# Four decoder layers on one core: moving the maxima of two attentions and the first block of two expert layers

## The chip, the cores and the metric

The kernel runs on one core of a Trainium2 chip. The metric is the device time of one execution in microseconds (us); several executions are made and their median is taken. The engines are TensorE (PE, its weight loads are shown as PEld), VectorE (DVE), ScalarE (ACT), GpSimd (POOL) and SyncE (SP, which only issues DMAs here). Each works through its own instructions in order and waits on semaphores for the others.

## The reference

`x` has 8 batches of 256 tokens with 128 features, `ctx` 8 batches of 1601 tokens with 64. Four layers of cross attention and feed-forward follow each other, each on the layer norm of x and added to it. Shortened:

```python
x = x + attention0(layernorm(x), ctx)   # 16 heads of 8, softmax over 1601 keys
x = x + ffn0(layernorm(x))              # attention among the 16 heads of a token, then a
                                        # mixture: sum over 8 experts e of gate[e] * (h2 @ We[e])
x = x + attention1(layernorm(x), ctx)   # 16 heads of 64
x = x + ffn1(layernorm(x))              # quantised linear, convolution of 3 taps, silu, linear
x = x + attention2(layernorm(x), ctx)   # one head of 128, no output projection
x = x + ffn2(layernorm(x))              # 8 experts, routed: sum of w[t,e] * down(silu(gate) * up)
x = x + attention3(layernorm(x), ctx)   # 16 heads of 8
x = x + ffn3(layernorm(x))              # 32 routed experts (8 of 32 a token) and a shared one
```

## The kernel before

All of it is one program of one core in five stages, written in the order in which each engine is to work: `attn0` (with ffn0 of batch 0 beside its last units), `wide` (attentions 1 and 2, with ffn0 of the other batches, ffn1 and the preparation of weights beside them), `experts` for ffn2, `attn3`, `experts` for ffn3.

**Attentions 0 and 3** are the function `narrow`. The work is 8 batches of 4 *units*, each unit being 4 heads of one batch; n counts the units, 0 to 31. A unit has 7 pairs of key chunks and two head groups, hence 14 *half steps*. In each, PE makes scores (`score`, L1011), ACT their exponentials (L1014), PE multiplies those of the step before with V (`values`, L1023). The softmax needs the maximum of every row beforehand: `maxima(n)` gives 14 tasks (`pair`), each two matmuls of a head pair's queries with a piece of the keys into banks of the pool `m` (three banks, L813) and two maximum reductions on DVE (L816); 2 of the 14 tasks are the short last pieces. A 15th task, `shift`, turns the maxima into a negated row; `place_shift(n)` transposes it on PE (L834) and has SP write it into Q (L838). `place(n, t)` has SP and POOL write K and Q of unit n into a ring of four. In unit n the tasks of unit n + 2 are spread over the 14 half steps; in unit 0 those of unit 1 come ahead of those of unit 2. The list `beside` holds other work with its place in the unit as a fraction.

Outside that list, at the end of `narrow`, the last batch's attention is divided by its sums, projected and added (`finish`, L846 to L854).

**Attentions 1 and 2** are the function `wide`: 272 jobs, 256 of attention 1 (32 a batch: 16 heads, 2 halves of the tokens) and 16 of attention 2 (2 a batch). A job n makes scores and maxima of n + 1, transposes the exponentials of n (`turn`), projects and adds n - 1, and multiplies the exponentials with v (`values`). Other work stands in `beside[n]`: what its steps have under "pe", "act0" and "dve" is issued ahead of `values`, what they have under "act" and "pool" behind it. The pool `m`, from which these steps and the queries take their PSUM, has one bank. ffn0 of batch b has 26 steps beside the 32 jobs of batch b - 1; its steps 22 to 25 are the mixture (four matmuls, and after each four multiply-adds of DVE into X, L1223). ffn1 of a batch follows in the next 32 jobs, that of batch 7 in jobs 256 to 266, one step a job. `prepare3` fetches the weights of ffn3 (`fetch`), turns them (`turn`, L1725) and writes them to DRAM, in jobs 27 to 31 of batches 1 to 6; `flip` and `maps2` are small transposes and maps that follow it there.

**The experts** work on 4 blocks k of 512 tokens. `prepare(k)` makes the layer norm, its transpose yT (L1613, L1615), the routing (L1619 to L1630, a sigmoid on ACT, many small DVE operations) and its transpose combT (L1634, L1636). `hidden(k, c)` makes gate and up of 128 hidden features (L1642, L1643), Silu on ACT and a product on DVE; six jobs later `weigh` (L1651) multiplies by the routing weights, and `down` (L1657) follows. For k = 0 `prepare` runs at the start of the stage, with its arithmetic on DVE; for the other blocks it runs beside the jobs of the block before.

Of the kernel before, what the change touches and what calls it, by code (L numbers as in the profile page):

```python
# [42 lines left out]
NB = 8  # L43
# [8 lines left out]
RING = 4  # L52
AFTER = 26
# [3 lines left out]
def decoder_kernel(ctx: ExitStack, tc: tile.TileContext, a: dict, out: bass.AP):  # L57
# [283 lines left out]


# [9 lines left out]
    def wide(layers, before, extra):  # L352
# [11 lines left out]
        with ExitStack() as es:  # L364
# [152 lines left out]
            beside = extra(es, A, B, bias)  # L517
# [114 lines left out]
    def narrow(wq, wkT, wvT, wo, bq, bk, bv, bo, first, after=None):  # L632
# [8 lines left out]
        with ExitStack() as es:  # L641
# [215 lines left out]
            class Scratch:  # L857

                PARTS = (("ct", KW), ("raw", NC * DC), ("nat", 512), ("nat", 512), ("k", 512), ("k", 512))
                SAME = dict(f0_h2="f0_h", f0_h2T="f0_hT", f0_mixT="f0_q", f0_y2="f0_dT")  # L860

                def __init__(self):
                    self.whole = [((one if t == "ct" else two).tile([P, n], F32, tag=t, name=f"left_{t}",
                                                                    bufs=1 if t in ("ct", "raw") else 2), n)
                                  for t, n in self.PARTS]
                    self.free = [n for _, n in self.PARTS]
                    self.at = {}

                def tile(self, shape, dt, tag=None, name=None, bufs=None):
                    n = 1  # L870
                    for x in shape[1:]:
                        n *= x
                    tag = self.SAME.get(tag or name, tag or name)
                    if tag not in self.at:

                        i = min((i for i in range(len(self.free)) if self.free[i] >= n), key=lambda i: self.free[i])
                        self.at[tag] = i, self.PARTS[i][1] - self.free[i], n
                        self.free[i] -= n
                    i, at, room = self.at[tag]
                    assert n <= room  # L880
                    t = self.whole[i][0][0:shape[0], at:at + n]
                    if len(shape) > 2:
                        axes = " ".join(f"a{x}" for x in range(len(shape) - 1))
                        t = t.rearrange(f"p ({axes}) -> p {axes}", **{f"a{x}": v for x, v in enumerate(shape[1:])})
                    return t
# [68 lines left out]
            more = maxima(1)  # L954
            for n in range(units):
                b, i = divmod(n, 4)
                v = V[b % 2]

                ms = []
                if n == 0:  # L960
                    ms += [*more[0], more[1]]
                if n + 2 < units:
                    pairs, shift = maxima(n + 2)
                    ms += [*pairs, shift]
                due = [len(ms) * (x + 1) // (2 * steps) for x in range(2 * steps)]
                done = 0
# [5 lines left out]
                if n + 1 < units:  # L972
                    beside.append((1.0 if n == 0 else 0.1, lambda: place_shift(n + 1)))
# [17 lines left out]
                if after is not None and n >= AFTER:  # L991
                    if n == AFTER:
                        late = after(Scratch(), bank)
                    per = 2 * steps
                    beside += [((x - per * (n - AFTER)) / per, lambda x=x: run([late[x]], EARLY + LATE))
                               for x in late if x // per == n - AFTER]
# [35 lines left out]
                for p in range(steps):  # L1032
                    e = two.tile([P, 4, 2, LQ], F32, tag="e", name="e")
                    for t in range(2):
                        score(p, t, e)
                        if before:
                            before.pop(0)()
                        while beside and (beside[0][0] * 2 * steps < 2 * p + t + 1 or p * t == steps - 1):
                            beside.pop(0)[1]()
                        for f in ms[done:due[2 * p + t]]:  # L1040
                            f()
                        done = due[2 * p + t]
# [22 lines left out]

    def attn3():
# [7 lines left out]
        with tc.tile_pool(name="w3", bufs=1) as p:  # L1074
# [4 lines left out]
            narrow(w3qT, flipped(0), flipped(1), w3oT, None, None, None, None, False)  # L1079


    def ffn0(p, b, bank=pm):
# [137 lines left out]

        def weigh(j, i):
            for e in range(4):
                nc.vector.scalar_tensor_tensor(X[b][:, j, :], t["pt"][:, e * D:(e + 1) * D],  # L1223
                                               t["gate"][:, j, 4 * i + e:4 * i + e + 1], X[b][:, j, :],
                                               ALU.mult, ALU.add)

# [4 lines left out]
        def exponent(name, s):  # L1231
# [21 lines left out]
                     dve=lambda: (inverse("gate"), combine(nc.vector, "gate", E, ALU.mult), weigh(0, 0))),  # L1253
        }
        for k, (j, i) in ((23, (0, 1)), (24, (1, 0)), (25, (1, 1))):
            steps[k] = dict(pe=lambda j=j, i=i: mixture(j, i), dve=lambda j=j, i=i: weigh(j, i))
# [48 lines left out]
    def ffn1(p, b):  # L1305
# [66 lines left out]
        def tanh():  # L1372
            t["th"] = p.tile([P, 4, LQ], F32, tag="f1_th", name="f1_th")
            nc.scalar.activation(t["th"], t["h"], AF.Tanh, scale=0.5)
# [33 lines left out]
        def done():  # L1408
            for j in range(QT):
# [7 lines left out]
                dict(pe=lambda: up(1), act0=lambda: middle(1), dve=lambda: sides(1)),  # L1417
                dict(act=tanh, pool=twice_silu),
# [8 lines left out]
    def besides(es, A, B, bias):  # L1427
# [9 lines left out]
        for n, f in zip(room, prepare3() + maps2(p, p, A[1], B[1], bias)):  # L1437
            at[n] = [dict(pe=f)]
        at[32 * (NB - 1) + 14] = at.get(32 * (NB - 1) + 14, []) + [dict(pool=lambda: big.update(sel2=select2()))]
# [100 lines left out]

    y0T = const.tile([P, LQ], F32, name="y0T")
# [23 lines left out]
    def experts(wr, n_r, route, n_e, wg, wu, wd, sel, shared):  # L1565
# [6 lines left out]
        with ExitStack() as es:  # L1572
# [4 lines left out]
            halves = [one.tile([P, T, P], F32R, name=f"halves{i}") for i in range(2)]  # L1577
            for t in halves:
                nc.vector.memset(t.bitcast(F32), 0.0)
# [4 lines left out]
            yT, combT, act, o = {}, {}, {}, {}  # L1584

            def prepare(k):

                fast = k == 0
                eng = nc.vector if fast else nc.gpsimd
                tokens = [X[2 * k + t // QT][:, t % QT, :] for t in range(T)]  # L1590
                st = p.tile([P, T, 6], F32, name="st")
                mv = p.tile([P, T, 2], F32, name="mv")
                var = p.tile([P, T], F32, name="var")
                for t in range(T):
                    nc.vector.bn_stats(st[:, t, :], tokens[t])
                if not fast:
                    yield
                for t in range(T):
                    nc.vector.bn_aggr(mv[:, t, :], st[:, t, :])
                nc.vector.tensor_scalar(var, mv[:, :, 1], 1e-5, None, ALU.add)  # L1600
                rs = guess(p, var, "ex_rs")
                refine(p, rs, var, "ex_t", eng)
                if not fast:
                    yield
                y = p.tile([P, T, D], F32, name="y")
                for t in range(T):
                    eng.tensor_scalar(y[:, t, :], tokens[t], mv[:, t, 0:1], rs[:, t:t + 1], ALU.subtract, ALU.mult)
                if not fast:
                    yield
                    yield  # L1610
                pt = pm()
                for t in range(T):
                    nc.tensor.transpose(pt[:, t * P:(t + 1) * P], y[:, t, :], ident)  # L1613
                yT[k] = p.tile([P, W], F32, name="yT")
                nc.scalar.copy(yT[k], pt)  # L1615
                yield
                pt = pm()
                for t in range(T):
                    nc.tensor.matmul(pt[:, t * n_r:(t + 1) * n_r], lhsT=yT[k][:, t * P:(t + 1) * P], rhs=wr,  # L1619
                                     start=True, stop=True)  # L1620
                s = p.tile([P, T, n_r], F32, name="s")
                nc.scalar.activation(s, pt[:, 0:T * n_r].rearrange("p (t n) -> p t n", n=n_r), AF.Sigmoid)
                yield
                for comb in route(p, s):
                    if comb is None:
                        yield
                h = halves[k % 2]
                hi, lo = h[:, :, 0:n_e], h[:, :, 32:32 + n_e]
                nc.gpsimd.tensor_copy(hi, comb)
                nc.gpsimd.tensor_tensor(lo, comb, hi.bitcast(F32), ALU.subtract)  # L1630
                yield
                pt = pm()
                for t in range(T):
                    nc.tensor.transpose(pt[:, t * P:(t + 1) * P], h[:, t, :].bitcast(F32), ident)  # L1634
                combT[k] = p.tile([P, W], F32R, name="combT")
                nc.scalar.copy(combT[k], pt)  # L1636
                yield

            def hidden(k, c):
                g, u, _, _ = chunks[c]  # L1640
                gu = ps2("gu")
                nc.tensor.matmul(gu[:, 0, :], lhsT=g, rhs=yT[k], start=True, stop=True)  # L1642
                nc.tensor.matmul(gu[:, 1, :], lhsT=u, rhs=yT[k], start=True, stop=True)  # L1643
# [4 lines left out]
            def weigh(k, c):  # L1648
                if chunks[c][3] is not None:
                    cm = pm()  # L1650
                    nc.tensor.matmul(cm, lhsT=chunks[c][3], rhs=combT[k], start=True, stop=True)  # L1651
# [24 lines left out]
            ahead = prepare(0)  # L1676
            while 0 not in yT:
# [122 lines left out]
```

## Time and profile before

| what | us |
|---|---|
| median of 3 runs | 3637.28 (3630.37 to 3639.38) |
| profiled execution | 3634.52, span 3632.8 |
| PE busy | 3431.8 (94% of the span) |
| DVE busy | 2602.2 (72%) |
| ACT busy | 2281.5 (63%) |
| POOL busy | 1129.4 (31%) |
| attention 0: first scores to end of last values | 49.0 to 731.4 |
| attentions 1 and 2: first scores to last projection | 766.1 to 2493.8 |
| experts of ffn2: first to last hidden and down | 2501.7 to 2702.4 |
| attention 3: first scores to end of last values | 2742.1 to 3395.3 |
| experts of ffn3: first hidden to last down | 3409.9 to 3627.5 |

A profile is of one execution. Its times start at the first instruction. A line of a timeline gives start, duration, engine, source line, operation, the tiles written and read, shapes and a count of merged instructions; in brackets stands how long the engine had been idle before, and which engine and line released it. The granted clock is the share of TensorE's full rate that the chip granted in a stretch. A busy PE is not a PE at full rate: matmuls overlap and their ends are modelled.

### The profile page before, as it was taken

How to read it: one execution, taken by the hardware profiler on the slowest of the kernel's cores; microseconds unless marked ns; L12 is line 12 of the kernel's file. 1: busy time of each engine (PE TensorE's matmuls, PEld its weight loads, DVE VectorE, ACT ScalarE, POOL GpSimd, SP SyncE). 2: the span in 40 equal slices, each digit the busy share in tenths (PEclk: the TensorE clock that was granted, in tenths of full speed). 3: DMA queues.
4: the chain of work that ended last, by engine and by line, in shares of the span. 5: the costliest groups of instructions: out<-in, count | busy, mean ns of one | idle time of the engine just before them, and what ended most of it. 6: DMA issues, size and time to landing. Idle time of an engine off the chain costs nothing.

```text
span 3632.8 us, 74838 instructions
## 1 busy us (share of the span) xinstructions
PE 3431.8 (94%) x28363; PEld 2315.0 (64%) x28363; DVE 2602.2 (72%) x6564; ACT 2281.5 (63%) x5685; POOL 1129.4 (31%) x2007
## 2 busy tenths in 40 slices
PE   7999999979999999999999999988999999999799
PEld 4555555458787877788777788865444555555344
DVE  6788888657777767767777777675556888889365
ACT  3788887746665656666676766653223878888422
POOL 5343444614152513333150502020123333332100
PEclk6899999989999999999999999998985999999899
DMA  4445444130001001000000000020013444443100
GB/s 93 73 76 76 68 70 62 24 81 2 15 2 32 1 24 38 1 27 1 15 1 15 1 15 1 11 69 18 0 24 52 74 65 70 65 64 51 44 3 9
DMA packets 112118, 130.21 MB, mean 36 GB/s; under 512 B 67184, under 2 KB 95888, under 8 KB 111120
## 3 DMA queue, kind: packets, MB, share of 16 engines
q1 hardware_dynamic: 91024, 114.09, 18.5%
q0 software_dynamic: 20480, 10.53, 1.2%
q8 instruction: 225, 3.69, 0.4%
q10 hardware_dynamic: 256, 0.82, 0.2%
q14 instruction: 133, 1.09, 0.1%
HBM read 44.79 MB, written 11.28 MB: 15 GB/s over the span
## 4 chain that ended last, share of the span: by engine, by line
PE 78%; DVE 10%; ACT 6%; POOL 2%; issue 2%; DMA 1%; ACTq 0%; SPq 0%; DVEq 0%; POOLq 0%
PE ov L1023 12%; PE o L476 11%; PE st L429 11%; PE pm L813 10%; PE t L462 8%; PE st L1011 6%; PE gu L1642 3%; PE gu L1643 3%; PE o L1657 3%; DVE mx L816 3%; ACT pt L464 2%; DVE ls L436 2%; ACT e L450 1%; PE st L784 1%; PE st L727 1%
## 5 line engine op out<-in xcount | busy, mean ns | idle before, releaser
L816 DVE TENSOR_REDUCE mx<-pm 128x1 f32<-128x512 f32 (+1 forms) x1792 | 1015.6, 627 | 212.7 <-PE pm L813 211.0
L1014 ACT ACTIVATE e<-st 128x512 f32<-128x512 f32 (+1 forms) x1792 | 916.0, 564 | 254.2 <-PE st L1011 198.6
L436 DVE TENSOR_REDUCE ls<-st 128x1 f32<-128x512 f32 x1088 | 549.5, 567 | 318.2 <-PE st L429 316.5
L450 ACT ACTIVATE e<-st,ls 128x512 f32<-128x512 f32 x1088 | 633.2, 601 | 13.4 <-DVE ls L439 12.6
L464 ACT COPY pt<-t 128x512 f32<-128x512 f32 x544 | 293.3, 586 | 460.3 <-PE t L462 459.6
L1023 PE MATMUL ov<-e,V 128*32 128x256 f32 x6656 | 556.2, 402 | 0.3 <-ACT e L1014 0.3
L813 PE MATMUL pm<-K,Q 64*128 64x512 f32 (+1 forms) x2048 | 529.1, 468 | 22.3 <-DVE mx L816 20.3
L462 PE MATMUL t<-ident,e 128*128 128x128 f32 (+1 forms) x3536 | 506.2, 281 | 2.4 <-ACT pt L464 0.2
L476 PE MATMUL o<-pt,v 128*64 128x128 f32 (+1 forms) x7072 | 493.8, 280 | 11.9 <-DVE pt L464 7.9
L813 PEld LDWEIGHTS pm<-K,Q 64*128 64x128 f32 x2048 | 238.9, 195 | 370.1 <-DVE mx L816 262.0
L476 PEld LDWEIGHTS o<-pt,v 128*64 128x64 f32 (+1 forms) x7072 | 416.2, 138 | 82.9 <-issue 31.6
L1011 PE MATMUL st<-Q,K 64*128 64x256 f32 (+1 forms) x3328 | 423.7, 296 | 2.6 <-DMA Q<-st 2.3
L462 PEld LDWEIGHTS t<-ident,e 128*128 128x128 f32 (+1 forms) x3536 | 391.5, 141 | 51.8 <-ACT pt L464 29.1
L429 PE MATMUL st<-ct,qh 128*128 128x512 f32 x1088 | 405.8, 373 | 1.6 <-ACT e L450 1.6
L1011 PEld LDWEIGHTS st<-Q,K 64*128 64x128 f32 (+1 forms) x3328 | 345.1, 188 | 44.7 <-issue 17.4
L429 PE MATMUL st<-ct,ql 128*128 128x512 f32 x1088 | 362.4, 366 | 0.0
L799 POOL DMA_DIRECT2D Q<-qh x256 | 128.0, 500 | 456.1 <-PE st L1011 417.8
L464 DVE COPY pt<-t 128x512 f32<-128x512 f32 (+1 forms) x544 | 239.0, 481 | 34.3 <-PE t L462 34.2
L429 PEld LDWEIGHTS st<-ct,qh 128*128 128x128 f32 x1088 | 205.2, 189 | 86.2 <-issue 38.2
L1645 ACT ACTIVATE act<-gu 128x512 f32<-128x512 f32 x132 | 78.8, 597 | 249.2 <-PE gu L1643 242.5
L450 ACT ACTIVATION_READ_ACCUMULATOR e<-st,ls 128x1 f32 x1088 | 230.8, 212 | 0.0
L429 PEld LDWEIGHTS st<-ct,ql 128*128 128x128 f32 x1088 | 206.0, 189 | 36.9
(456 smaller groups left out, 4192.9 us busy)
## 6 DMA issues: line engine op xcount, KB each, us to landing
K<-kh SPq DMA_DIRECT2D x252, 100.1 KB
K<-kl SPq DMA_DIRECT2D x252, 100.1 KB
ct<-ctd SPq DMA_DIRECT2D x24, 801.0 KB
ctd<-ct SPq DMA_DIRECT2D x8, 801.0 KB
v<-in_ctx SPq DMA_DIRECT2D x16, 384.0 KB
Q<-qh POOLq DMA_DIRECT2D x256, 16.0 KB, 2.6
Q<-ql POOLq DMA_DIRECT2D x256, 16.0 KB, 2.7
raw<-in_ctx SPq DMA_DIRECT2D x8, 384.0 KB
```

What stands on the lines that cost most here:

```text
L429: nc.tensor.matmul(st[n, c][:, 0:w], lhsT=q[k, h][i][:, j * P:(j + 1) * P], rhs=ct[k][:, at:at + w], start=(i == 0), stop=(i == 1))
L436: nc.vector.tensor_reduce(ls[n][:, c:c + 1], st[n, c][:, 0:BANK[c][1]], AX.X, ALU.max)
L450: nc.scalar.activation(e[n][:, at:at + w], st[n, c][:, 0:w], AF.Exp, bias=ls[n][:, 4:5], scale=1.0, accum_out=ls[n][:, 5 + c:6 + c])
L462: nc.tensor.transpose(t[0:m, (c - 4 * i) * P:(c - 4 * i + 1) * P], e[n][:, c * P:c * P + m], ident)
L464: (nc.scalar.copy if i < 2 else nc.vector.tensor_copy)(p[0:m, 0:w], t[0:m, 0:w])
L476: nc.tensor.matmul(o[n][half, 0:P], lhsT=v[k][0:m, c, :], rhs=turned[n, c // 4][0:m, (c % 4) * P:(c % 4 + 1) * P], start=(c < 2), stop=(c ...
L799: nc.gpsimd.dma_start(out=q[r:P:8, :].bitcast(F32), in_=qhl[b][r % 2][src, :].bitcast(F32))
L813: nc.tensor.matmul(pt[g][:, x * w:(x + 1) * w], lhsT=q[r, j * P:(j + 1) * P], rhs=k[r, at:at + w], start=True, stop=True)
L816: nc.vector.tensor_reduce(mx[:, js[0]:js[-1] + 1, 2 * t + g, at // 512], pt[g][:, 0:len(js) * w].rearrange("p (j k) -> p j k", k=w), AX.X, ...
L1011: nc.tensor.matmul(st[g][0:m, j, :], lhsT=k[r, c * P:c * P + m], rhs=q[r, :], start=True, stop=True)
L1014: nc.scalar.activation(e[0:m, 2 * t + g, 0:len(cs), :], st[g][0:m, 0:len(cs), :], AF.Exp)
L1023: nc.tensor.matmul(cell["o"][32 * g:32 * g + 32, :], lhsT=v[0:m, at:at + 32], rhs=e[0:m, g, c % 2, :], start=(c == 0), stop=(c == NC - 1))
```

## The change

Six edits are made together.

1. The tasks of `maxima(m)` are spread, one pair a half step, over the 14 half steps that end with the eighth of unit m - 1; those of unit 1 over the first eight of unit 0. `place_shift(m)` moves from a tenth of unit m - 1 to its tenth half step.
2. `prepare` becomes a function outside `experts`. For block 0 of ffn2 it runs beside jobs 260 to 271 of `wide` (attention 2), one step a job; for block 0 of ffn3 beside half steps 52 to 80, counted from unit 26, of attention 3, every other one. Both put yT and combT into tiles of their own, and use the POOL where the old start used DVE.
3. Of the four products of each mixture step, ACT makes two (copies with a scale), which POOL adds to each other and to X.
4. The tanh of ffn1 is made in two halves, the first one job earlier.
5. `prepare3` puts the small flips and `maps2` between `fetch` and the turns that need what it fetched.
6. `Scratch`, which hands out parts of unused tiles, takes the tiles as an argument.

```diff
+DONE = 8
...
-            beside = extra(es, A, B, bias)
+            beside = extra(es, A, B, bias, bp)
...
+            per = 2 * steps
+            tasks = {}
+            def plan(m):
+                pairs, shift = maxima(m)
+                first_, last_ = max(0, per * (m - 2) + DONE), per * (m - 1) + DONE
+                for x, f in enumerate(pairs):
+                    tasks.setdefault(first_ + (last_ - first_) * x // len(pairs), []).append(f)
+                tasks[last_ - 1].append(shift)
+            plan(1)
             for n in range(units):
-                ms = []
-                if n == 0:
-                    ms += [*more[0], more[1]]
                 if n + 2 < units:
-                    pairs, shift = maxima(n + 2)
-                    ms += [*pairs, shift]
-                due = [len(ms) * (x + 1) // (2 * steps) for x in range(2 * steps)]
+                    plan(n + 2)
...
-                    beside.append((1.0 if n == 0 else 0.1, lambda: place_shift(n + 1)))
+                    beside.append(((DONE + 1) / per, lambda: place_shift(n + 1)))
...
-                        late = after(Scratch(), bank)
+                        late = after(left(), bank)
...
-                        for f in ms[done:due[2 * p + t]]:
+                        for f in tasks.pop(per * n + 2 * p + t, []):
                             f()
...
+    def first_block3(p, bank):
+        return {per: step for per, step in zip(range(52, 84, 2), first_block(p, routing3, bank))}
...
-            narrow(w3qT, flipped(0), flipped(1), w3oT, None, None, None, None, False)
+            narrow(w3qT, flipped(0), flipped(1), w3oT, None, None, None, None, False, first_block3)
...
+        def weighted(j, i):
+            w = t["mixed"] = p.tile([P, 2, D], F32, tag="f0_mixed", name="mixed")
+            for e in range(2):
+                at = 4 * i + e
+                nc.scalar.activation(w[:, e, :], t["pt"][:, e * D:(e + 1) * D], AF.Copy,
+                                     scale=t["gate"][:, j, at:at + 1])
         def weigh(j, i):
-            for e in range(4):
+            for e in range(2, 4):
...
+        def add_weighted(j):
+            w = t["mixed"]
+            nc.gpsimd.tensor_tensor(w[:, 0, :], w[:, 0, :], w[:, 1, :], ALU.add)
+            nc.gpsimd.tensor_tensor(X[b][:, j, :], X[b][:, j, :], w[:, 0, :], ALU.add)
...
-                dict(pe=lambda: up(1), act0=lambda: middle(1), dve=lambda: sides(1)),
-                dict(act=tanh, pool=twice_silu),
+                dict(pe=lambda: up(1), act0=lambda: middle(1), dve=lambda: sides(1), act=lambda: tanh(0)),
+                dict(act=lambda: tanh(1), pool=twice_silu),
...
-        for n, f in zip(room, prepare3() + maps2(p, p, A[1], B[1], bias)):
+        for n, f in zip(room, prepare3(maps2(p, p, A[1], B[1], bias))):
             at[n] = [dict(pe=f)]
+        n = bp.tile([P, 2048], F32, tag="f0_pr", name="left_pr")
+        for x, step in enumerate(first_block(Scratch([(n, 2048)]), routing2)[:12]):
+            at.setdefault(32 * NB + 4 + x, []).insert(0, step)
...
+    def first_block(p, routing, bank=pm):
+        h = p.tile([P, T, P], F32, name="halves")
+        gen = prepare(p, 0, routing, h, dict(yT=yT0, combT=combT0), bank)
+        return [dict(dve=lambda: nc.vector.memset(h, 0.0))] + [dict(pe=lambda: next(gen, None)) for _ in range(16)]
...
-            ahead = prepare(0)
-            while 0 not in yT:
-                next(ahead)
+            ahead = iter(())
...
-                for _ in range(2 if i < LAG else 1):
-                    next(ahead, None)
+                next(ahead, None)
...
+        flips = [lambda: flip(wr3, wr3r)] + [lambda i=i: flip(shr[:, i, :], shr[:, i, :]) for i in range(3)]
+        between = [flips[0:3], [flips[3], *more[0:2]], more[2:4]]
         parts = [selection, lambda: fetch(0)]
         for n in range(3):
+            parts += between[n]
             for c in range(0, 16, 4):
                 parts.append(lambda n=n, c=c: (turn(n, c), c == 12 and n < 2 and fetch(n + 1)))
-        parts.append(lambda: flip(wr3, wr3r))
-        parts += [lambda i=i: flip(shr[:, i, :], shr[:, i, :]) for i in range(3)]
```

## The prediction

> **What bounds the kernel now.** I read the page's slices first. TensorE (PE) is busy in nearly all of them, yet its granted clock dips in four places.
>
> ```profile
> PE   7999999979999999999999999988999999999799
> ...
> PEclk6899999989999999999999999998985999999899
> ```
>
> These are the first units of attentions 0 and 3 (slices 1 and 30) and the starts of the two expert layers (slices 28 and 38). The windows of the first units show the price: unit 0 of attention 0 runs 47 to 104 us, wholly at half clock; a later unit takes 17.5 us.
>
> ```profile
> 47.00:106.00 59.00, 53.85 (x249) 26.28 (x249) 32.83 (x62) 21.91 (x44) 19.32 (x31) 0.50 0.23 43
> 106.00:131.00 25.00, 24.73 (x222) 14.27 (x220) 17.55 (x32) 17.21 (x35) 5.42 (x13) 0.83 0.37 49
> ...
> 2824.00:2841.00 17.00, 17.00 (x188) 9.14 (x188) 15.89 (x32) 14.16 (x30) 7.18 (x17) 1.00 0.53 71
> ```
>
> Columns: stretch, length, then PE, PEld, DVE, ACT, POOL busy (x instructions), clock, DMA. The last three units of attention 3 show the other end:
>
> ```profile
> 3347.00:3364.50 17.50, 17.50 (x193) 9.26 (x190) 16.57 (x32) 14.66 (x32) 0.00 (x0) 1.00 0.02 7
> 3364.50:3380.50 16.00, 15.78 (x163) 7.46 (x163) 1.92 (x3) 14.21 (x31) 0.92 (x2) 1.00 0.03 9
> 3380.50:3395.30 14.80, 14.69 (x148) 6.52 (x147) 0.00 (x0) 13.26 (x28) 0.00 (x0) 1.00 0.02 6
> ```
>
> Units 30 and 31 have no maxima: DVE idles and ACT sets the pace. So unit 0 carries 28 pairs of maxima, and units 30 and 31 none. PE's timeline of unit 0 (two pairs a half step, first three lines) and of unit 1 (one pair) gives the price of the second pair:
>
> ```profile
> 2757.66 1.22 PE L813 MATMUL pm<-K,Q 64*128 64x512 f32 x3
> 2759.24 0.79 PE L813 MATMUL pm<-K,Q 64*128 64x512 f32 x1 [0.36 <-DVE mx L816]
> ...
> 2761.40 1.22 PE L813 MATMUL pm<-K,Q 64*128 64x512 f32 x3
> ...
> 2804.16 0.79 PE L813 MATMUL pm<-K,Q 64*128 64x512 f32 x2
> ...
> 2806.32 0.79 PE L813 MATMUL pm<-K,Q 64*128 64x512 f32 x2
> ```
>
> 3.73 us from 2757.66 to 2761.40 against 2.16 us, both at half clock: 1.57 us. The fourth matmul waits for a bank that DVE still reads. Where the short last piece is the second pair the step takes 3.18 us (2754.48 to 2757.66), so it costs 1.0. Last, the start of the first expert layer:
>
> ```profile
> 2493.33 0.49 PE L490 MATMUL o<-B,os 128*128 128x128 f32 x2 [0.36 <-ACT os L486]
> 2499.81 1.15 PE L1613 MATMUL pm<-ident,y 128*128 128x128 f32 x4 [5.99 <-DVE y L1607]
> 2501.68 2.08 PE L1642 MATMUL gu<-yT,wg 128*128 128x512 f32 x2 [0.72 <-ACT yT L1615]
> ...
> 2516.26 0.66 PE L1634 MATMUL pm<-ident,halves 128*128 128x128 f32 x4 [3.79 <-POOL halves L1630]
> ...
> 2523.60 1.02 PE L1642 MATMUL gu<-yT,wg 128*128 128x512 f32 x2
> ```
>
> Idle, then half clock, then a wait for the routing: six jobs take from 2501.68 to 2523.60. At full clock a job takes 1.71 us (2521.89 to 2523.60).
>
> **Part by part.**
>
> *Starts of attentions 0 and 3.* Unit 0 falls from 28 pairs to 14 + 6. The eight that leave are the last eight of the second map, six full and two short: 6 x 1.57 + 2 x 1.0 = 11.4 us less, if the clock stays half. From half step 8 (the first is 0) there is one pair a step. In both attentions the clock rose 9.4 us after the single pairs began (2798.4 to 2807.8; 105.2 to 114.6). If it does so now, the rest of unit 0 (six steps of 2.16, three key parts of 1.2, 0.6 for the shift: 17 us, less 9.4) runs at double speed, 3.8 less, and unit 1 takes its usual 20.8 instead of 24.9, 4.1 less: 19.3 in all. Ends 11.4 and 19.3; I take 15, between them, since it is not shown that single pairs alone raise the clock. Twice: **-30**.
>
> [...]
>
> *Their ends.* The eight pairs reappear in unit 30. A pair costs (17.48 - 14.82)/14 = 0.19 us there, as ACT paces: 1.5 us. In attention 0, unit 30 also carries ffn0's steps, so up to a pair's 0.43 us on PE (3.4): **+2.5**. Shift and its place keep two half steps between them (before 13 and 1 of the next unit, now 7 and 9).
>
> *Attention 3's end, with block 0 of the last experts* (half steps 52 to 80). DVE, at 16.6 of 17.5 us until unit 30's eighth step, gets the memset (0.51), statistics (0.81), aggregates and guess (0.9): 2.2, of which I put 1.5 on the path. ACT, which paces, gets two copies (0.58 each), the sigmoid (0.28) and two table loads (1.28 each): 4.0. POOL gets refine and y, on no one's path. With the 1.5 for pairs: **+7**, ends 4 and 10 (ffn0's 26 steps at the end of attention 0 cost 17.8 us over the same units of attention 3 and make the upper end, 0.7 a step).
>
> *Attention 2 with block 0 of the first experts.* Each step stands ahead of ffn1's in its job, and `pm` has one bank. In job 265 ffn1's `turn_r(1)` (2448.30) waits for the copy of yT, behind the exponentials that end at 2449.8: +2.1. In job 266 `down` (2454.08) waits for the sigmoid, behind exponentials that end at 2456.15, a load of 1.28 and 0.21: +3.6. Batch 7's chain runs through both, so both count. DVE's small operations of jobs 268 to 270 (some 1.2 us each) lie in its 1.35 us gap after L482. POOL's refine (3.3 us, like batch 7's) stands in job 262 behind a later batch's own, and is done before job 264 needs POOL. With 1.3 for what slips: **+7**, ends 3 and 10.
>
> [...] Here the load at 3414.31 follows an activation that ended at 3414.30, and the sigmoid starts at 3415.60: 1.28, no drain. [...]
>
> *Start of the first experts.* No transposes, no wait: the first hidden job follows the last projection (2493.8) at full clock, and the seventh starts six jobs on, at 2504.1 instead of 2523.6: **-19.5**. With half clock for 8.8 us (as at 2501.68 to 2510.4) it is -15. The Silu table load hides behind the first matmuls.
>
> *Start of the last experts.* Today the first job starts at 3409.88, the seventh at 3435.20. Then the weights are next: issued at 3401.53, when the last projection frees the memory; two first pieces of 256 KB land by about 3405.3 (512 KB at the 193 GB/s of 3402 to 3405). PE has idled, so 8.8 us at half clock (2.6 jobs of 3.42) and 3.4 of 1.71: seventh at 3420. **-15**; ends -8 (pieces late) and -16.5.
>
> *Fetches.* PE waits 4.9 us for `raw_up`, then runs at half clock to 1360.5: the values take 3.25 instead of 1.74, and with the transposes some 2.5 is lost; the wait for `raw_gate` is 2.2. The new order leaves over 20 jobs ahead of `raw_up` and two (12 us) ahead of `raw_down`, both longer than the 4.9 + one job that 1 MB needed. **-9**, ends -7 and -10. SP's next user is a batch load 16 jobs on.
>
> *Mixture and tanh.* Jobs 22 to 25 take 0.94 and 1.24 us more than their neighbours; 0.86 is the matmul, and the odd jobs' extra 0.37 is the wait for `ql`. So DVE's four multiply-adds (0.35 each) are hidden, and halving them gains nothing. ACT gets 0.6 us in a job where it idles 1.7 before L464. Were that idle gone, 28 jobs x 0.6 = 17 us; I allow 3. POOL's two adds come before the next job's multiply-adds on the same rows, some 4 us later. Tanh: the same 1.1 us in two. **0**, ends -1 and +3.
>
> Sum: -30 + 2.5 + 7 + 7 - 19.5 - 15 - 9 = **-57**. The profiled execution took 3634.5 (span 3632.8 and 1.7 around it): 3577.5. The median of the runs is 2.8 above it: **3580**.
>
> **Rivals.**
> 1. *Late shifts, slower.* The negated maxima now leave at half step 9, five steps (6.2 us) ahead of the first scores that need them, in SP's order behind eight copies of K. The place is the start of 62 units; a us late costs 62. It decides from 57/62 = 0.9 us; at 1.5 us late: 3673. For it: attention 0's units of the fourth kind send 400 + 384 + 400 KB ahead, which end some 13.5 us into 17.5. Against it: at 2740.26 issue to use took 1.9 us, and in unit 29 the K issues end 9 us after the unit starts, before step 9 at 11.3. 6%.
> 2. *The clock stays half as long as before*: 11.4 for 15, twice, 3587. For it: unit 0 still begins with double pairs. 14%.
> 3. *The hoisted steps stall their hosts* twice as much (+28 for +14): 3594. For it: job 267 waits 5.7 us on the same in-order chain. 10%.
> 4. *Block 0 isn't what holds the experts* (memory or weights are): only the routing waits of 3.8 and 5.6 and the slow clock after each (3 + 3) go: -15 for -34.5, 3600. Against it: DVE writes `halves` 0.06 us after the last add, so memory is free. 6%.
>
> My forecast has 62%, 2% is left for no change. **Range**: all gains at their good ends (-38.6, -19.5, -16.5, -10, -1) and costs at their low ones (1, 4, 3) make -78; the other ends (-22.8, -15, -8, -7; 4, 10, 10, 3) -26: 3560 to 3611. I give 3557 to 3612, which holds rivals 2 to 4. 0.3% is 10.9 us, about what a measurement can tell. Faster 0.91, same 0.03, slower 0.06.
>
> **What would show it.** Right: the clock up within unit 0; unit 1 near 20.8 us; unit 30 at 17 to 18; no wait at the routing transposes before the first experts, the seventh job some 10.5 us after the last projection; no wait for `raw_up`. Wrong: PE waiting for Q from the shift at unit starts (rival 1), unit 1 still at 24.9 (2), jobs 265 to 271 over 7 us longer (3), hidden's first matmul late after the last projection (4).

## The result, and the profile after

The changed kernel takes 3572.44 us in the median of 4 runs (3569.32 to 3574.68). Before takes 3636.06 beside it, and the ratio is 0.9822 [0.981, 0.9834]: 64 us faster, where 57 were forecast. The profiled execution took 3569.3 (span 3567.6), 65.2 less than the one before.

The two slices that the prediction read first, now from the page of the changed kernel:

```profile
PE   7999999979999999999999999988999999999899
...
PEclk9999999989999999999999999999996999999999
```

Of the four dips of the clock that the prediction named, the one at attention 3 (slice 31, which the prediction counted as 30) is left; the small one in slice 9 is in both kernels. The digits say less than they seem to. No step of the clock is on record before 82.8 us in this execution, and the matmuls ahead of it have the durations of half clock (two of L841 take 0.79 us at 78.39 and 0.50 at 83.57); and a 9 stands for 90% or more, so that the half clock from 3349.4 to 3363.0, at the start of the last experts, does not show. Attention 3 is recorded whole. Its windows (stretch, length, then PE, PEld, DVE, ACT, POOL busy, clock, DMA share, GB/s):

```profile
2702.00:2743.00 41.00, 38.91 (x228) 19.34 (x230) 25.24 (x45) 18.57 (x39) 13.39 (x23) 0.60 0.22 46
2743.00:2764.10 21.10, 21.10 (x218) 12.49 (x218) 16.48 (x32) 16.62 (x35) 4.61 (x11) 1.00 0.48 92
3291.00:3309.00 18.00, 17.63 (x184) 8.87 (x184) 16.78 (x34) 13.75 (x29) 0.00 (x0) 1.00 0.03 7
3309.00:3331.00 22.00, 19.71 (x186) 10.10 (x188) 18.47 (x70) 17.30 (x34) 6.38 (x18) 0.92 0.02 6
3331.00:3348.00 17.00, 16.24 (x164) 7.36 (x156) 2.23 (x14) 15.00 (x31) 0.76 (x2) 1.00 0.02 5
```

Unit 0 takes 41 us for 57, unit 1 has the full clock throughout, and the last three units are no longer 17.5, 16.1 and 14.8 but 18.9, 22.9 and 15.5. PE's timeline in unit 0:

```profile
2725.86 0.79 PE L841 MATMUL pm<-K,Q 64*128 64x512 f32 x1 [0.36 <-DVE mx L844]
...
2731.34 0.80 PE L841 MATMUL pm<-K,Q 64*128 64x512 f32 x2
...
2734.89 0.52 PE L841 MATMUL pm<-K,Q 64*128 64x512 f32 x2
```

The last wait for a bank is at 2725.86, single pairs begin at 2731.34, and from 2735.0 on the clock is full (0.52 us for 0.80). The starts of the two expert layers:

```profile
2472.76 1.12 PE L1689 MATMUL gu<-yT,wg 128*128 128x512 f32 x2
2473.73 0.38 PE L518 MATMUL o<-B,os 128*128 128x128 f32 x2
...
2484.68 1.02 PE L1689 MATMUL gu<-yT,wg 128*128 128x512 f32 x2
...
3351.97 1.55 PE L880 MATMUL st<-w3oT,ot 128*128 128x128 f32 x4 [4.62 <-POOL ot L875]
3357.06 2.05 PE L1689 MATMUL gu<-yT,w 128*128 128x512 f32 x2 [3.54 <-DMA w<-w3d]
...
3370.60 1.02 PE L1689 MATMUL gu<-yT,w 128*128 128x512 f32 x2
```

The first experts begin ahead of the last projection (L518) and have no wait for the layer norm or the routing. The last experts wait for their weights alone.

The sum by stages, from the traces of the two profiled executions (units end with the copy `os` on ACT, jobs of `wide` with the copy of their tail):

| stage | before | after | difference | forecast |
|---|---|---|---|---|
| units 0 and 1 of attention 0, from the first scores | 81.6 | 62.1 | -19.5 | -15 |
| units 0 and 1 of attention 3 | 81.6 | 61.8 | -19.8 | -15 |
| units 2 to 25, both attentions | 948.2 | 951.6 | +3.4 | 0 |
| units 26 to 31 of attention 0 | 122.2 | 122.3 | +0.1 | +2.5 |
| units 26 to 31 of attention 3 | 102.9 | 111.9 | +9.0 | +7 |
| jobs 1 to 255 | 1590.5 | 1581.9 | -8.6 | -9 |
| jobs 256 to 271 | 125.4 | 132.2 | +6.8 | +7 |
| last job of attention 2 to the last hidden of the first experts | 198.0 | 179.0 | -19.0 | -19.5 |
| end of attention 3 to the last hidden of the last experts | 220.9 | 203.6 | -17.3 | -15 |

The rest (first scores, the passages between stages, the end) makes -0.3.

### The profile page after: what moved, and what is told of

It is laid out like the page before. It is cut to its first block, busy times and chain, and to the rows that moved or that the text cites. A ratio compares the mean times of both kernels' runs of the same rounds, so it can differ in the third digit from the quotient of the medians.

```text
span 3567.6 us, 74943 instructions
## 1 busy us (share of the span) xinstructions
PE 3401.5 (95%) x28363; PEld 2305.4 (65%) x28363; DVE 2578.8 (72%) x6470; ACT 2296.6 (64%) x5757; POOL 1173.1 (33%) x2103
## 3 DMA queue, kind: packets, MB, share of 16 engines
q1 hardware_dynamic: 91024, 114.09, 17.9%
## 4 chain that ended last, share of the span: by engine, by line
PE 81%; DVE 9%; ACT 6%; issue 2%; POOL 1%; DMA 1%; ACTq 0%; SPq 0%; POOLq 0%; DVEq 0%
PE ov L1032 13%; PE o L504 12%; PE st L457 12%; PE pm L841 11%; PE t L490 8%; PE st L1020 6%; PE gu L1689 3%; PE gu L1690 3%; PE o L1704 3%; ACT pt L492 3%; DVE mx L844 2%; DVE ls L464 2%; ACT e L478 2%; PE st L812 1%; PE st L755 1%
## 5 line engine op out<-in xcount | busy, mean ns | idle before, releaser
L1032 PE MATMUL ov<-e,V 128*32 128x256 f32 x6656 | 572.3, 397 | 0.3 <-ACT e L1023 0.3
L841 PE MATMUL pm<-K,Q 64*128 64x512 f32 (+1 forms) x2048 | 512.2, 460 | 15.2 <-DVE mx L844 13.2
L841 PEld LDWEIGHTS pm<-K,Q 64*128 64x128 f32 x2048 | 234.1, 191 | 335.3 <-DVE mx L844 226.9
L1020 PE MATMUL st<-Q,K 64*128 64x256 f32 (+1 forms) x3328 | 411.6, 291 | 4.0 <-DMA Q<-st 2.3
L1020 PEld LDWEIGHTS st<-Q,K 64*128 64x128 f32 (+1 forms) x3328 | 339.5, 186 | 38.6 <-issue 10.5
L492 DVE COPY pt<-t 128x512 f32<-128x512 f32 (+1 forms) x544 | 239.1, 481 | 34.8 <-PE t L490 34.7
L1032 PEld LDWEIGHTS ov<-e,V 128*32 128x32 f32 x6656 | 143.3, 108 | 155.1 <-issue 42.1
```

The lines of the kernel that those rows point to most:

```text
L492: (nc.scalar.copy if i < 2 else nc.vector.tensor_copy)(p[0:m, 0:w], t[0:m, 0:w])
L841: nc.tensor.matmul(pt[g][:, x * w:(x + 1) * w], lhsT=q[r, j * P:(j + 1) * P], rhs=k[r, at:at + w], start=True, stop=True)
L1020: nc.tensor.matmul(st[g][0:m, j, :], lhsT=k[r, c * P:c * P + m], rhs=q[r, :], start=True, stop=True)
L1032: nc.tensor.matmul(cell["o"][32 * g:32 * g + 32, :], lhsT=v[0:m, at:at + 32], rhs=e[0:m, g, c % 2, :], start=(c == 0), stop=(c == NC - 1))
```

## The experiments

Their stages in one table (us). "Starts" are units 0 and 1 of attentions 0 and 3, "tail" units 26 to 31 of attention 3, "hosts" jobs 265 to 271, "seventh" the time from the end of attention 2, and of attention 3, to the seventh hidden job.

| kernel | time | starts | tail | hosts | seventh |
|---|---|---|---|---|---|
| before | 3634.5 | 81.6, 81.6 | 102.9 | 51.0 | 30.3, 39.5 |
| changed | 3569.3 | 62.1, 61.8 | 111.9 | 59.4 | 11.5, 22.8 |
| e1 maxima alone | 3595.3 | 61.9, 61.2 | 105.2 | 50.0 | 29.6, 37.7 |
| e2 no block 0 beside attention 2 | 3580.8 | 61.8, 61.4 | 113.2 | 50.0 | 29.6, 22.9 |
| e3 no block 0 beside attention 3 | 3583.2 | 61.3, 61.9 | 105.3 | 62.4 | 11.5, 37.8 |
| e4 small edits undone | 3585.5 | 61.8, 61.7 | 115.1 | 59.3 | 11.5, 22.8 |
| e5 maxima to half step 10 | 3568.4 | 54.8, 55.9 | 113.5 | 59.4 | 11.5, 22.9 |
| e6 maxima to half step 12 | 3856.0 | 59.5, 55.7 | 137.8 | 62.4 | 11.5, 22.8 |
| e7 steps moved | 3567.5 | 61.5, 61.1 | 114.1 | 53.6 | 11.5, 22.7 |
| e8 sigmoid by exponentials | 3570.6 | 61.5, 61.1 | 110.6 | 57.9 | 11.5, 23.0 |
| e9 combined | 3554.3 | 58.7, 57.9 | 110.6 | 53.6 | 11.5, 23.0 |
| e10 combined, exponentials, step 11 | 3581.4 | 69.0, 68.9 | 107.7 | 53.6 | 11.5, 22.9 |
| e11 changed, again | 3570.0 | 61.6, 62.3 | 111.9 | 60.5 | 11.5, 22.7 |
| e12 combined, exponentials | 3558.2 | 58.7, 58.2 | 107.7 | 53.6 | 11.5, 22.9 |

Each time is that of the execution profiled; e1 to e8 have this one alone, and executions of one kernel differ by up to 9 us (before) or 5 (changed). Some places vary by 1 to 5 us between executions of the same instructions: jobs 261 to 263, the hosts (59.3 in e4 to 62.4 in e3), the passage into attention 3 (50.2 to 55.0), and the tail (111.9 twice, 113.2 in e2, 115.1 in e4; by how often and how long the clock falls in it, as e8 below shows).

**e1.** In the kernel before:

```diff
+first_, last_ = max(0, per * (m - 2) + DONE), per * (m - 1) + DONE   # DONE = 8
-(1.0 if n == 0 else 0.1, lambda: place_shift(n + 1))
+((DONE + 1) / per, lambda: place_shift(n + 1))
```

> The kernel before with edit 1 alone (maxima end with the eighth half step, place_shift at the tenth). Theory (the parts add up, and each start gains by fewer double pairs and by an earlier full clock): each of the two attentions' first two units are 19 to 20 us shorter, the clock rises inside unit 0; units 2 to 25 cost 0 to 3 us more, units 30 and 31 of attention 3 about 1.5 more (eight pairs at 0.19): about -36, 3599 us. Rival A (the clock is not part of it; the doubled pairs are all): 11.4 each, unit 1 still at 24.9: -20, about 3614. Rival B (the later shift makes each unit start wait): 24 steady units of each attention 0.9 us longer or more, no gain.

Measured: 3595.3, and 3631.1 for before beside it: -35.8. The starts fall by 19.7 and 20.4, the clock rises inside unit 0, units 2 to 25 of attention 3 grow by 2.9 and its tail by 2.3. Rival A, which is rival 2 of the prediction, falls: unit 1 takes 21.1. So does rival B, for the 24 units 2 to 25 grow by 0.4 and 2.9 in all, not by 0.9 each. The small steady loss belongs to this edit.

**e2 and e3** make block 0 at the start of its expert layer again, the one for the first layer, the other for the last:

```diff
-act, o, made = {}, {}, {0: dict(yT=yT0, combT=combT0)}
+act, o, made = {}, {}, {0: {}}
+ahead = prepare(p, 0, routing, halves[1], made[0], pm, True)
```

> The changed kernel, but block 0 of the first experts is made at the start of that stage again. Theory: jobs 256 to 271 fall from 125.4 back to 118.6 us, the seventh hidden job comes 19 to 20 us later after the last projection: +13, about 3582 us. Rival (it was not the making of block 0 that held the experts, but the weights or the memory): the hidden jobs start as early as in the changed kernel, or less than 12 us later, and the kernel gets faster by the 7 us in the hosts.

> The changed kernel, but block 0 of the last experts is made at the start of that stage again. Theory: the start of the last experts takes 17 us more; units 26 to 31 of attention 3 fall by some 8 of the 9.1 us that they had gained, since the eight pairs moved into unit 30 cost 0.2 to 1.5: +8 to +9, about 3581 us. Rival (the tail of attention 3 grew by the pairs of maxima that unit 30 now carries, not by block 0's steps): units 26 to 31 stay within 3 us of the changed kernel's, so +15 or more, 3587.

e2: the seventh hidden job comes 18.0 us later, the hosts fall by 9.4: 3580.8. e3: the seventh comes 15.0 later and the jobs behind it take another 1.0; the tail falls by 6.6 to what e1 has: 3583.2. Both theories hold in their places, though not in every number: e2 has 122.0 for jobs 256 to 271, where 118.6 was expected, and e3 loses 13.9 us for 8 to 9, since its hosts took 3.0 and its passage into attention 3 took 4.8 longer, neither of which the edit touches. PE's timeline of e3 at the last experts shows the same two waits as before, and the weights are not in them:

```profile
3357.93 1.15 PE L1612 MATMUL pm<-ident,y 128*128 128x128 f32 x4 [6.42 <-DVE y L1606]
...
3379.24 1.12 PE L1634 MATMUL pm<-ident,halves 128*128 128x128 f32 x4 [5.62 <-POOL halves L1630]
```

Rival 4 of the prediction falls with these two. And of the 9.0 us by which the tail grew, 2.3 are the pairs' (e1) and 6.6 block 0's.

**e4** undoes edits 3, 4 and 5:

```diff
-dict(pe=lambda: up(1), act0=lambda: middle(1), dve=lambda: sides(1), act=lambda: tanh(0)),
-dict(act=lambda: tanh(1), pool=twice_silu),
+dict(pe=lambda: up(1), act0=lambda: middle(1), dve=lambda: sides(1)),
+dict(act=tanh, pool=twice_silu),
...
-            for e in range(2, 4):
+            for e in range(4):
...
-            parts += between[n]
```

> The changed kernel with edits 3, 4 and 5 undone (mixture on DVE alone, tanh in one piece, fetches next to their turns). Theory: the jobs of batch 2 (64 to 95) are 8 us longer with waits for raw_up and raw_gate; mixture jobs 22 to 25 unchanged (6.25 and 7.03 us); jobs 261 and 262 together 1.6 us longer: +10, about 3582 us. Rival (the halved mixture gains, or the tanh hides more): jobs 22 to 25 of the batches 0.3 us or more longer each (28 jobs, +8), so +18.

Measured: 3585.5. Jobs 1 to 255 take 1591.2 for 1581.9, most of it in batch 2 (208.1 for 200.2). Its view of PE's waits has two lines that the changed kernel's lacks (us in total, times, longest):

```profile
PE pm L1754 <- DMA raw_up<-in_L_ffn_w_up: 4.8, 1, 4.8
...
PE pm L1754 <- DMA raw_gate<-in_L_ffn_w_gate: 1.8, 1, 1.8
```

The mixture's jobs take 6.25 and 7.03 in both kernels: nothing, as forecast. Jobs 261 and 262 differ by 1.2 and 0.3, no more than they vary by, so no effect of the tanh is shown. Of the 16 us, 3.2 are the tail and 2.5 the passage into `wide`, which this kernel does not touch.

**e5 and e6** change one number, `DONE = 8` to 10 and to 12.

> The changed kernel with the maxima ending two half steps later (the tenth half step; four double pairs in unit 0 instead of six; the shift is placed at the twelfth, three half steps or 3.7 us ahead of the first scores). Theory: the shift still arrives (1.9 us from issue to use in the profile before), units 2 to 25 unchanged within 2 us; unit 0 loses two pairs at half clock, 2.5 us an attention, and two more pairs stand in unit 30 (0.2 each): -2 to -5, about 3566 us. Rival 1 of the prediction (late shifts): waits of PE for Q at unit starts of 0.3 us or more, 62 of them, +19 or more.

> The changed kernel with the maxima ending at the twelfth half step and the shift placed at the last one, 1.25 us ahead of the first scores. Theory: 1.9 us from issue to use is longer than that, so PE waits for Q at every unit start for 0.6 us or more, the loss that rival 1 of the prediction named, 62 x 0.6 = +37 at the least, less 5 for unit 0: about 3600 us or more. Rival (something else hides it, such as the values of the step before, which PE makes first): no waits, -4 to -8 from unit 0.

e5: the starts give another 7.3 and 5.9, more than expected, but units 2 to 25 lose 4.8 and 2.9 and the two tails 2.5 and 1.6: 3568.4, no gain worth the name. e6: 3856.0. The waits of PE, e5 first:

```profile
PE st L1020 <- DMA Q<-st: 6.7, 8, 2.3
```

```profile
PE st L1020 <- DMA Q<-st: 128.3, 63, 4.7
```

One of e5's eight is the prologue's 2.3; seven are new, 0.6 each on average. With 6.2 us between shift and scores (the changed kernel) there is none, with 3.7 some, with 1.25 all of them, 2.0 each. The loss in e6 is 287 us, over twice the waits, for the clock falls to half behind them: its mean is 0.919 (0.980 in the changed kernel), and in attention 3, where Q is waited for at 2900.75, 2923.32 and 2945.82, the matmuls of a pair take 0.79 us together in the stretch that follows each wait and 0.50 later. Rival 1 of the prediction is a real cliff; the change stands two to four half steps away from it.

**e7** moves block 0's steps within their hosts.

```diff
-for x, step in enumerate(first_block(Scratch([(n, 2048)]), routing2)[:12]):
-    at.setdefault(32 * NB + 4 + x, []).insert(0, step)
+for job, count in ((260, 1), (261, 1), (262, 1), (263, 2), (267, 1), (268, 1), (269, 2), (270, 2), (271, 1)):
...
-zip(range(52, 84, 2), first_block(p, routing3, bank))
+zip((61, 4, 12, 20, 21, 30, 40, 62, 64, 66, 68, 70, 72, 74, 77), first_block(p, routing3, bank))
```

> The changed kernel with block 0's steps moved within their hosts. In attention 2 the transposes and the routing go from jobs 265 and 266 to 267 and 268, where no step of ffn1 stands; in attention 3 the memset, statistics, norm, transposes and sigmoid go into units 26 to 28, where ACT has 2.8 us to spare a unit, and DVE's routing stays in units 30 and 31. Theory (what costs is the place: PE waits for ACT behind the sigmoid's loads where ACT paces): jobs 265 and 266 return to 8.6 and 6.2 us, jobs 267 to 271 grow by 1 to 4: -4 to -7; unit 30 falls from 22.9 to under 19, units 26 to 28 grow by 0.5 each: -2 to -5. About 3562 us. Rival (the steps cost as much anywhere, since PE and DVE are full in units 26 to 29): the same 9 us in attention 3, and the 8 us reappear in jobs 267 to 271.

The theory holds in attention 2: the hosts fall from 59.4 to 53.6, with jobs 265 and 266 back at 8.6 and 6.2 and the five behind them 2.5 longer. In attention 3 the rival holds: 114.1, within what the tail varies by, with 1.7 more in unit 26 and 3.1 more in unit 28, and unit 30 at 21.3, not under 19. A step among maxima costs there whatever the unit, so ACT's spare time was not the point.

**e8** asks whether ACT's table loads were.

```diff
-nc.scalar.activation(s, logits, AF.Sigmoid)
+nc.scalar.activation(s, logits, AF.Exp, scale=-1.0)
+nc.vector.tensor_scalar(s, s, 1.0, None, ALU.add)
+nc.vector.reciprocal(s, s)
```

> The changed kernel with block 0's sigmoid made as 1 / (1 + exp(-x)) in both hosts, in the places that they have: no switch of ACT's table, two more small DVE operations. Theory (the two loads of 1.28 us in each host make PE wait, and the wait drops the clock): job 266 falls from 12.5 by 2 to 5 us, unit 30 from 22.9 by 3 to 5 us and the clock stays full in it: -5 to -10, about 3562 us. Rival (the steps' arithmetic and their PSUM banks cost it, not the loads): units 26 to 31 within 1.5 us of the changed kernel's 111.9, job 266 within 1.

Job 266 falls by 2.35, within the theory. The tail falls by 1.3 only, where the rival stands, and the whole is no faster. In the changed kernel, unit 30's fall of the clock does stand behind the loads. Its timeline:

```profile
3321.72 1.28 ACT L1623 ACT_TABLE_LOAD   x1 [0.52 <-PE st L1620]
...
3323.30 1.28 ACT L1023 ACT_TABLE_LOAD   x1
...
3325.25 0.62 PE L1020 MATMUL st<-Q,K 64*128 64x256 f32 x3 [1.45 <-ACT e L1023]
```

PE waits 1.45 us for the exponential behind the two loads, and the clock falls at 3325.5. (e2, e4 and e11 have the same wait, with a fall behind it.) In e8 this wait is gone, but its timeline where unit 30 starts shows another fall in its place:

```profile
3308.84 0.28 DVE L1594 BATCH_NORM_STATS2 left_k<-x 128x6 f32<-128x128 f32 x1
...
3309.76 0.50 PE L841 MATMUL pm<-K,Q 64*128 64x512 f32 x1 [0.36 <-DVE mx L844]
...
3311.42 0.37 DVE L1598 BATCH_NORM_AGGREGATE left_k<-left_k 128x2 f32<-128x6 f32 x4
...
3312.66 0.50 PE L841 MATMUL pm<-K,Q 64*128 64x512 f32 x1 [0.61 <-DVE mx L844]
```

Statistics and aggregates stand among the reductions on DVE, PE waits twice for a bank, 0.97 us together, and the clock is at half from 3313.1 to 3316.5 without any table load. The changed kernel, e11, e4 and e2 have the same two waits at this place; behind them the clock falls in e2 (from 3321.5, for 3.4 us) and stays up in the other three. So the 1.3 is one fall against another. e2, with both falls, has the like of e8: 113.2 to 110.6, so the loads and the fall behind them cost 2.6, and the fall that e8 shares with e2 costs 1.3 (e2 against the changed kernel).

**e9 to e12** put this together: attention 2 as in e7, attention 3's steps behind half step 62 (maxima over, DVE idle, which also takes refine and y from the POOL), and only unit 1's maxima later. e10 and e12 add e8's exponentials; e10 ends unit 1's maxima one half step later still. e11 is the changed kernel beside them.

```diff
+FIRST = 10                                        # e10: 11
+ends = {k: per * (k - 1) + (FIRST if k == 1 else DONE) for k in (m - 1, m)}
+at = (63, 64, 65, 66, 67, 69, 70, 72, 73, 74, 75, 76, 77, 78, 81)
```

> The changed kernel with three moves. (a) Attention 2's steps where e7 had them. (b) In attention 3 all of block 0's steps behind half step 62, when the maxima are over and DVE idles, with refine and y on DVE. (c) The maxima of unit 1 alone end at the tenth half step, those of unit 2 are spread over the next twelve. Theory (what DVE gets while maxima are pending makes PE wait and costs clock; the steady loss of e5 came from the later shift, its gain from unit 0): jobs 256 to 271 some 4 us shorter than in the changed kernel; units 26 to 31 fall from 111.9 to 106 to 108; units 0 and 1 of each attention 6 to 8 shorter and units 2 to 25 within 1.5: -20 in all, about 3550 us, ratio to before 0.977. Rival (the tail's cost is ACT's sigmoid loads and copies where ACT paces, so units 30 and 31 suffer more): units 26 to 31 at 112 or more; and if unit 0's earlier end is given back by the maxima of unit 2, units 0 to 3 gain nothing: 3567.

> As the combined kernel, with the sigmoid made by exponentials (no table loads in the hosts) and unit 1's maxima ending at the eleventh half step, its shift placed two half steps (about 2.5 us) ahead of the first scores. Theory: units 0 and 1 another 1 to 3 us shorter an attention if the shift is there in time, and behind the maxima, where ACT paces, the two loads cost their 2.6 us, so units 30 and 31 are 2 to 2.6 shorter; jobs 266 to 271 1 to 2 shorter: -5 to -8 against the combined kernel, about 3544. Rival (the lead is too short): PE waits for Q at the start of unit 1 for 0.5 us or more and the clock falls back: the starts lose 3 or more each and the kernel is no faster.

> The changed kernel once more, beside the two combined ones on the same chip, as their measure: 0.9822 of before within its interval (0.981 to 0.9834), 3568 to 3575 us. Units 26 to 31 of attention 3 tell how much the tail varies between executions (111.9, 113.2 and 115.1 so far with the same steps).

> The combined kernel (unit 1's maxima ending at the tenth half step) with the sigmoid made by exponentials in both hosts. Theory: units 0 and 1 as in the combined kernel (58.7 and 57.9 us from the first scores), since the loss of the other one was the eleventh half step; units 26 to 31 of attention 3 at 107.7 for 110.6, the two loads saved where ACT paces; jobs 256 to 271 unchanged at 127.5: -3, about 3556 us, ratio 0.979. Rival (by chance of the clock, the starts fall back here too, as one wait can do it): units 0 and 1 at 65 or more.

| kernel | median of runs | lowest to highest | ratio to before |
|---|---|---|---|
| e11 changed, again | 3572.36 | 3570.02 to 3574.32 | 0.983 [0.9816, 0.9843] |
| e9 | 3559.13 | 3554.27 to 3563.45 | 0.9797 [0.9784, 0.9811] |
| e10 | 3570.44 | 3550.86 to 3581.75 | 0.9825 [0.9798, 0.9852] |
| e12 | 3558.17 | 3554.64 to 3559.53 | 0.979 [0.9777, 0.9803] |

e9 beats both kernels, the changed one by 13.2 us where 20 were expected: the hosts give 5.8, the starts 3.4 and 3.9 (6 to 8 expected; unit 0 gives 4.7 and 5.1, but unit 1, with one pair of unit 2 more, takes 22.4 for 21.1), and the tail 1.3, at 110.6 and not the 106 to 108 expected. There the sigmoid's loads now stand where ACT paces, and e12 shows their price in that place: 110.6 to 107.7 (e10 has 107.7 too), so 2.9 for two loads of 1.28, with a half clock from 3317.2 to 3320.6 in e9 that e12 lacks. The new form of the steps is worth 2.9 too: 110.6 in e8 against 107.7 in e12, both without loads, of which 1.3 is the fall that e8 shares with e2. How much of the other 1.6 is the place and how much the move from POOL to DVE, no run tells. e12's median is 1 us below e9's, less than the two spread.

e10 fails by its eleventh half step, in which alone it differs from e12. PE's timeline at the start of attention 0's unit 1:

```profile
81.37 0.50 PE L1022 MATMUL st<-Q,K 64*128 64x256 f32 x4 [0.39 <-DMA Q<-st]
83.65 0.50 PE L842 MATMUL pm<-K,Q 64*128 64x512 f32 x1 [0.55 <-DVE mx L845]
```

Two waits, 0.94 us together, and the clock falls at 84.3 and stays at half until 111.6. Unit 1 takes 34.7 for e9's 22.4, in attention 3 likewise. The other runs of e10 lie at 3551, 3568, 3570 and 3582; that these are executions in which the clock fell in neither, one or both attentions fits roughly, at 12 us a fall, but only one was profiled.

## Why the prediction was right

The forecast of 3580 rested on seven terms. All but one (the end of attention 0) had their sign and place; 3572.4 lies 7.6 below, mostly by one term.

- **Starts, -30: mis-sized, -39.3 measured.** I took 15, between 11.4 and 19.3, as it was not shown that single pairs raise the clock. The clock rose under them: unit 0 fell by 15.7 and 16.1 and unit 1 by 3.8 and 3.7, where the good end had 15.2 and 4.1. It rose 4.4 us after the single pairs began in attention 0 (78.39 to 82.8) and 3.6 after in attention 3 (2731.34 to 2735.0), not 9.4: 5.0 and 5.8 us sooner than before's. Counted from the last wait for a bank it was 9.9 and 9.1 us, and 11.6 and 11.7 before; so the stretch that I had measured can as well be counted from the last double pair's wait, and which of the two counts is not shown.
- **Ends of the attentions.** Attention 0: +2.5 forecast, 0.1 measured. Attention 3: +7 forecast, 9.0 measured. The pairs cost 2.3 for 1.5 (e1), block 0 6.6 (e3) for my 4.0 for ACT and 1.5 for DVE. Of the 6.6, 2.6 go with the loads (e2 to e8), another 1.6 with the form of the steps that e12 has, and 2.4 stay; each is from one or two executions. I had priced the loads at their own 2.6. The size came out, but by another path: PE waited 1.45 us, and 3.4 us at half clock followed, which the sum lacked.
- **Units 2 to 25** were costed at nothing and took 3.4 more, 2.7 of it in attention 3; e1 ties it to the maxima's new places. No wait of PE explains it: in attention 3, PE's idle time in these units falls from 2.4 to 1.2 us while its busy time grows from 466.8 to 470.6. Why it is busy for longer stays open.
- **Attention 2, +7**: 6.8 measured. Job 265 gave 2.1 as forecast, job 266 gave 6.2 for 3.6. The mechanism is the forecast one, but the wait of PE behind the load was followed by half clock (2431.2 to 2438.0), which the sum lacked. The changed kernel's timeline in job 266:

```profile
2429.84 1.28 ACT L1623 ACT_TABLE_LOAD   x1
2431.13 0.21 ACT L1623 ACTIVATE left_pr<-pm 128x48 f32<-128x48 f32 x1
...
2431.39 1.97 PE L1433 MATMUL pm<-w2T,f_rT 128*128 128x128 f32 x8 [2.80 <-ACT left_pr L1623]
```

 `down` (L1433) waits 2.80 us, and its eight matmuls take 1.97. That the total fits is in part luck: jobs 265 and 266 gave 8.3, and the other fourteen fell by 1.5, in places that vary by as much (e11, the same kernel, has 134.5 for 132.2). The load begins at 2429.84, when the exponential before it has ended (2429.82), and the sigmoid at 2431.13, when the load has (2431.12): nothing but its 1.28 us stands between them.
- **First experts, -19.5**: the seventh job starts 11.0 us after the last projection where 10.5 was forecast; -19.0 by the last hidden.
- **Last experts, -15**: -17.3, a little past the good end of -16.5. The clock rose 6.0 us after the first job for 8.8, and the weights landed 5.1 us after the last projection began.
- **Fetches, -9, and mixture and tanh, 0**: -8.6, no change in the mixture (e4), and none shown for the tanh.

Rival 1, named as decided from 0.9 us, did not occur, but e6 shows it to be real and dearer than its 62 units times the wait. Rivals 2 and 4 fell with e1, and with e2 and e3. Rival 3 fell by its price, since the two hosts lost 15.8 us where it had 28; yet the sign that I had named for it is there, as jobs 265 to 271 are 8.4 us longer (59.4 for 51.0), over the 7 that I allowed. And one sign of being right is missing: unit 30 of attention 3 takes 22.9 us, not 17 to 18; with the pairs alone (e1) it takes 17.9.

## What to carry to other kernels

Price a short wait of PE by what the clock does behind it, not by its length: here waits of 0.9 to 2.8 us in all were followed by 3.4 to 27.3 us at half clock. Work moved beside a host belongs where the engine that it needs has nothing on the way to PE, which is a matter of half steps: block 0's steps without table loads cost 5.3 us among the maxima, some 4 without the fall that came by chance, and 2.4 behind them (e8 and e12 against the tail of e3). The in-order chain with a DMA at its end had a cliff here, and two runs with the lead cut from 6.2 us to 3.7 and 1.25 showed where it is.

## What the hardware showed that was not expected

The stretches at half clock in these runs have lengths near whole multiples of the shortest, 3.4 us: 3.4, 6.8, 10.2, 13.6 and 27.3 (3325.5 to 3328.9, 2431.2 to 2438.0, 649.4 to 659.7 and 3349.4 to 3363.0 in the changed kernel; 84.3 to 111.6 in e10). The same wait did not cost the same in two executions: unit 30's fall, behind a wait of 1.45 us in both, lasts 3.4 us in the changed kernel and 13.6 in e4, with the same steps. And not every wait counts: in e9 the clock rose at 2713.1, 3.7 us after a wait of 0.36, and waits of 0.55 and 0.56 that followed within 8 us did not lower it; and the two waits of 0.36 and 0.60 where unit 30 starts, the same in five executions, lowered it in e2 and e8 and not in the changed kernel, e4 and e11.
